# FFN's products in halves, at other addresses, and grouped with the attention's products

## The chip, the core and the metric

The kernel runs on one core of a Trainium2 chip, in one launch. The metric is the device time of a run in microseconds, the median of several runs. Before the change it is 484.53 us (three runs, 483.99 to 485.03). Besides the timed runs there is one profiled execution, with a trace of every instruction; all durations below come from that trace.

## The reference

One transformer layer over x of 4 x 2048 tokens of 256 features, in float32, cut to what is computed:

```python
Q, K, V = x @ W_q.T, x @ W_k.T, x @ W_v.T
# chunks of 32 tokens; mask[i, j] = decay ** (i - j) for i >= j, else 0
S = einsum('bncd,bnkd->bnck', Qc, Kc) * mask
O = einsum('bnck,bnkd->bncd', S, Vc)
x = layernorm(x + ((sigmoid(x @ W_g.T) * O) @ W_o.T + x))
# FFN: integer weights times 1/127, 768 hidden features
gate, up = x @ wg.T, x @ wu.T
x = layernorm(x + (silu(gate) * up) @ wd.T)
```

## The kernel before

**Blocks and passes.** The 8192 tokens are cut into 16 blocks of `TB` = 512. Features lie in `KD` = 2 groups of 128 partitions, hidden features in `KH` = 6 chunks of 128. The main loop (L1173) makes one pass for each of blocks 0 to 13. A pass works on three blocks at once: the FFN of block b, attention's values and output of block n = b + 2, and projections and scores of block m = b + 3. Passes 1 to 12 take the branches marked `late`; passes 0 and 13 take the others, and the last two blocks have code of their own behind the loop.

**Products in parts.** Float32 operands are split into a high part of the type float32r (a float32 format of TensorE) and a rest. FFN's rests are fp16: a chunk of FFN is a sum of high x high (float32r) and rest x rest (fp16) products. They are written in `ffn_pieces` (L912), which returns three functions: the high products, the low products, and one that issues silu on ScalarE (L937) and gives back another that issues the multiplication by the up projection on VectorE (L948), the copy to float32r on ScalarE (`u_hi`, L953) and the rest on GpSimd (`u_lo`, L954). The gate and the up projection of a chunk take a PSUM bank each, two products for each kind and projection: the weights are stationary, 128 x 128, and h's transposed block `hT` moves, 512 columns. All products of FFN's up part stand in one line, L923; `fg<-hT_hi,fg_hi` is a high product of the gate, `fu<-hT_lo,fu_lo` a low one of the up projection. `ffn_up` (L965) calls the three functions for whole chunks.

The attention's four projections (gate `p_g`, value `p_v`, scores `p_y`, output `p_o`) have three float32r terms: high, low, and, after ScalarE has scaled the bank, a third ("gap"). `three` (L535) writes them: for each of two banks the high and the low products and ScalarE's scaling (L542), and later, when the function that it returns is called, the third term and what takes the bank away (`finish`). Two helpers write the products. `feature_major` (L495, its products L501) has stationary weights and moves 512 columns of tokens; it serves `split_gate` (L555, finish is a tanh) and `split_y` (L563, finish is a copy to `yT` on VectorE, L567). `token_major` (L513, L523) has stationary tokens and moves the weights' 256 columns; it serves `split_v` (L571) and `split_out` (L824). FFN's down projection `fdn` (L764, in `project_back_late`, L755) also moves 256 columns of weights against stationary tokens, float32r for the high and fp16 for the low part.

The parts of the tokens come from `pieces_of_tokens` (L464): high on ScalarE, low on GpSimd, gap on VectorE; `token_parts` (L488) calls it and hands back the gap's part as a function. `split_h` (L890) makes `hT_hi` (ScalarE) and `hT_lo` (GpSimd) of a normalized block which `move_h` (L867) has transposed with VectorE and 16 DMAs on SyncE's queue.

The scores (`attn_scores`, L647, products L663) are many products of 128 x 32 tiles of the array, and the values (`attn_values`, L708, products L699) are 64 of 64 x 64 tiles; VectorE then multiplies the values by the gate into `goT` (L718).

**What sets the order.** Nearly every instruction goes through `in_turn`, which keeps the written order on its engine; the order of the calls in the loop's body is the order of work on TensorE, ScalarE and VectorE. PSUM's 8 banks are one ring that is handed out in the written order. Addresses in SBUF come from the tile pools: each pool is one stretch, and the pools follow each other in the order in which they are opened (L101 to L113). In the built program before, every weight's high part lies at an address with remainder 192 modulo 256 bytes, and the tokens' parts (`hT_hi`, `u_hi`, the parts of x and of `goT`) at remainder 0.

TensorE's order in a late pass before the change (numbers are FFN's chunks):

```
low 0, low 1, high 0, high 1 | y: high and low | high 2, low 2 | y: third
high 3, low 3 | scores (L663) | values (L699) | low 4, low 5, high 4
gate: high and low | value: high and low | gate: third | high 5 | value: third
output: high and low | down: high of chunks 0, 1 | output: third | down: high of 2 to 5, low
```

Of the kernel before, what the change touches and what calls it, by code (L numbers as in the profile page):

```python
# [48 lines left out]
F32R = mybir.dt.float32r  # L49
# [5 lines left out]
P = 128  # L55
# [3 lines left out]
TB = 512  # L59
NG = TB // P  # L60
HB = TB // 2
# [15 lines left out]
def kernel(  # L77
# [18 lines left out]
    KD = D // P  # L96
# [2 lines left out]
    assert NB > 3  # L99

    const = ctx.enter_context(tc.tile_pool(name="const", bufs=1))  # L101
    setup = ctx.enter_context(tc.tile_pool(name="setup", bufs=2))
    xin = ctx.enter_context(tc.tile_pool(name="xin", bufs=2))
    work = ctx.enter_context(tc.tile_pool(name="work", bufs=2))
# [5 lines left out]
    sums = ctx.enter_context(tc.tile_pool(name="sums", bufs=1))  # L110
    small = ctx.enter_context(tc.tile_pool(name="small", bufs=8))
    tiny = ctx.enter_context(tc.tile_pool(name="tiny", bufs=1))
    psum = ctx.enter_context(tc.tile_pool(name="psum", bufs=8, space=bass.MemoryType.PSUM))  # L113

    def in_turn(ins):
        tc.keep_in_program_order(ins)

    def bank(name):
        return psum.tile([P, TB], F32, tag="ps", name=name)
# [156 lines left out]
    def integers(w, w_int, name):  # L276

        k, n = w.shape[0] // P, w.shape[1]
        both = [
            const.tile([P, k, n], dtype, tag=f"{name}_{kind}", name=f"{name}_{kind}")  # L280
            for kind, dtype in (("hi", F32R), ("lo", F16))
        ]

        def cast(kind, which=range(len(w_int))):
            for i in which:
                in_turn(nc.scalar.copy(pieces_of(both[kind], i), w_int[i]))

        return both, cast
# [199 lines left out]
    def token_parts(t, name):  # L488
        parts, high, low, difference = pieces_of_tokens(t, name)
        for k in range(KD):  # L490
            high(k)
            low(k)
        return parts, lambda: [difference(k) for k in range(KD)]

    def feature_major(a, b):  # L495

# [347 lines left out]
    def transpose_h(b, h, up=H_UP):  # L844

        up = H_UP / up
        hi = work.tile([P, KD, TB], F32R, tag="hT_hi", name=f"hT_hi_{b}")
        lo = work.tile([P, KD, TB], F16, tag="hT_lo", name=f"hT_lo_{b}")
        for dc in range(KD):
            pt = bank(f"pt_{b}_{dc}")  # L850
            for g in range(NG):
                in_turn(
                    nc.tensor.transpose(
                        pt[:, g * P : (g + 1) * P], h[:, g, dc * P : (dc + 1) * P], ident
                    )
                )
            in_turn(nc.scalar.mul(hi[:, dc, :], pt, up))
            in_turn(
                nc.vector.scalar_tensor_tensor(
                    lo[:, dc, :], pt, up, hi[:, dc, :].bitcast(F32), ALU.mult, ALU.subtract  # L860
                )
            )
        return hi, lo
# [24 lines left out]
        return hT  # L888

    def split_h(b, hT):  # L890
        hi = work.tile([P, KD, TB], F32R, tag="hT_hi", name=f"hT_hi_{b}")
        lo = work.tile([P, KD, TB], F16, tag="hT_lo", name=f"hT_lo_{b}")
        for dc in range(KD):
            whole = hT[:, dc, :, :].rearrange("p q (g t) -> p g q t", g=NG)
            in_order = [
                part[:, dc, :].rearrange("p (g q t) -> p g q t", g=NG, q=NQ)
                for part in (hi, lo)
            ]
            tc.keep_in_program_order(nc.scalar.copy(in_order[0], whole))  # L899
            nc.gpsimd.tensor_tensor(  # L900
                in_order[1], whole, in_order[0].bitcast(F32), ALU.subtract
            )
        return hi, lo
# [4 lines left out]
    def no_more_splits():  # L908
        while late_splits:
            late_splits.pop(0)()  # L910

    def ffn_pieces(b, hT, uT, hc, cols=slice(0, TB)):  # L912

        n = cols.stop - cols.start
        pg = bank(f"fg_{b}_{hc}_{cols.start}")[:, :n]
        pu = bank(f"fu_{b}_{hc}_{cols.start}")[:, :n]
        fresh = [pg, pu]

        def products(kind):
            for i, (pb, w) in enumerate(((pg, fg), (pu, fu))):  # L920
                for dc in range(KD):
                    for part in [cols]:
                        product = nc.tensor.matmul(  # L923
                            pb[:, part.start - cols.start : part.stop - cols.start],
                            lhsT=w[kind][:, dc, hc * P : (hc + 1) * P],
                            rhs=hT[kind][:, dc, part],
                            start=len(fresh) > 1 - i,
                            stop=True,
                            skip_group_check=True,
                        )  # L930
                        in_turn(product)
                        if len(fresh) > 1 - i:
                            fresh.pop()

        def activate():
            s = work.tile([P, n], F32, tag="s", name=f"s_{b}_{hc}")
            in_turn(nc.scalar.activation(s, pg, AF.Silu, scale=SCALE / H_UP))  # L937
            no_more_splits()
            if len(uT[0]) == hc:
                for kind, dtype, tiles in zip(("hi", "lo"), (F32R, F16), uT):  # L940
                    tiles.append(
                        acts.tile([P, TB], dtype, tag=f"u_{kind}", name=f"u_{kind}_{b}_{hc}")
                    )

            def multiply():
                u = work.tile([P, n], F32, tag="u", bufs=3, name=f"u_{b}_{hc}")
                in_steady_turn(
                    nc.vector.scalar_tensor_tensor(u, pu, U_UP / H_UP, s, ALU.mult, ALU.mult)  # L948
                )
                hi, lo = uT[0][hc][:, cols], uT[1][hc][:, cols]  # L950

                def split():
                    in_steady_turn(nc.scalar.copy(hi, u))  # L953
                    in_steady_turn(nc.gpsimd.tensor_tensor(lo, u, hi.bitcast(F32), ALU.subtract))  # L954

                if lagging:
                    late_splits.append(split)
                else:
                    split()

            return multiply

        return lambda: products(0), lambda: products(1), activate
# [209 lines left out]
    for b in range(NB - 2):  # L1173
# [13 lines left out]
        def pieces(hc):  # L1187
            return ffn_pieces(b, hT, uT, hc)
# [3 lines left out]
        if late:  # L1192
            (high_0, low_0, silu_0), (high_1, low_1, silu_1) = pieces(0), pieces(1)
            low_0()
            low_1()
            high_0()
            silu_0()()
            high_1()
            multiply = silu_1()
        else:  # L1200
            if b:
                up_now(b, hT, uT, 0)
            multiply = ffn_up(b, hT, uT, range(1, 2), held=True)
# [11 lines left out]
            multiply()  # L1215
        if not more:
            goT = attn_values(n, sT, v, sg)
        multiply = ffn_up(b, hT, uT, range(2, 3), held=True)
        if b > 1:
            normalize(r_before, *scales_out, range(NG // 2))  # L1220
        multiply()
# [13 lines left out]
        if more:  # L1235
            sT_next = attn_scores(m, yT)
            goT = attn_values(n, sT, v, sg)
            if late:
                (high_4, low_4, silu_4), (high_5, low_5, silu_5) = pieces(4), pieces(5)
                low_4()  # L1240
                low_5()
                go_parts, go_gaps = token_parts(goT, f"go_{n}")
                high_4()
                silu_4()()
                go_gaps()
                sg_next, g_rest = split_gate(m, x_parts)
                v_next, v_rest = split_v(m, x_parts)
                gate = g_rest(hold=True)
                if m + 1 < NB:
                    x_parts, x_high, x_low, x_difference = pieces_of_tokens(  # L1250
                        xTs[m + 1], f"x_{m + 1}"
                    )
                    for k in range(KD):
                        x_high(k)
                high_5()
                multiply = silu_5()
                v_copies = v_rest(hold=True)
                gate()
                multiply()
                if m + 1 < NB:  # L1260
                    for k in range(KD):
                        x_difference(k)
            else:
                multiply = ffn_up(b, hT, uT, range(4, 5), held=True, low_first=True)
                go_parts, go_gaps = token_parts(goT, f"go_{n}")
                cast_fd(1, range(1))
                multiply()
                go_gaps()
                v_next, v_rest = split_v(m, x_parts)
                sg_next, g_rest = split_gate(m, x_parts)  # L1270
                v_rest()
                cast_fd(1, range(1, 2))
                up_with_cast(b, hT, uT, 5, 1, range(2, 3))
# [352 lines left out]
    with tc.If(wide_any > 0, preferred_fallthrough_block=False):  # L1626
# [1 line left out]
        homes = [  # L1628
            pool.tile([P, KD, TB], F32, tag=tag, name=f"wide_{i}")
            for i, (pool, tag) in enumerate(  # L1630
                ((work, "hT_hi"), (work, "hT_hi"), (sums, "x_hi"), (sums, "x_lo"))
            )
        ]
        last_home = work.tile([P, TB], F32, tag="hT_lo", name="wide_last")
# [58 lines left out]
```

## Time and profile before

| | before |
|---|---|
| median of 3 runs | 484.53 us |
| profiled execution, its own time | 485.13 us |
| its span, first to last instruction | 483.5 us |
| granted TensorE clock, mean | 0.997 of full speed |
| ScalarE / VectorE / GpSimd busy | 370.3 / 343.2 / 279.2 us |
| matmul instructions | 3704, of them 736 float32r of 512 columns and 1120 of 256 |

How to read what follows. The page gives, for each engine, the busy time, its share of the span and the number of instructions; then the chain of work that ended last, followed back from the last instruction. The timeline has a line for each run of equal instructions: start in us from the span's start, time to the end of the last one, engine, source line, operation, output<-inputs, tile of the array, shape, type and count; a float32r product is listed as f32. Products overlap in the array: a product's own duration in the trace (some 0.28 us for 256 columns, 0.4 for 512) is longer than the distance from its start to the next one's. So the cost of products on TensorE is read from start to start, and two runs in the timeline overlap by the last product's tail.

### The profile page before, as it was taken

To read this page: it belongs to the slowest core of one execution; us is meant where nothing else is said; L and a number is where in the kernel's file an instruction comes from. 1 tells how busy PE (TensorE), PEld (TensorE's weight loads), DVE (VectorE), ACT (ScalarE), POOL (GpSimd) and SP (SyncE) were. 2 spreads that over 40 slices of the span, in tenths; PEclk is the share of its full clock that TensorE was granted. 3 is DMA by queue.
4 is the path that set the end of the run, shared out by engine and by line. 5 is a ranking of instruction groups with operands and counts; after the bars stand their busy time and mean duration, and the time that the engine had idled before them with its cause. 6 is when DMAs were issued, how large, how long until landed. Compare 5 with 4: busy or idle time off the path is not lost.

```text
span 483.5 us, 12279 instructions
## 1 busy us (share of the span) xinstructions
PE 477.2 (99%) x4760; PEld 380.8 (79%) x4760; DVE 343.2 (71%) x795; ACT 370.3 (77%) x699; POOL 279.2 (58%) x285
## 2 busy tenths in 40 slices
PE   9999999999999999999999999999999999999995
PEld 5788787787978879697787978878697787968674
DVE  4587958776777766858676777866858676677656
ACT  4878788587877778788786887778788786786845
POOL 2835755655655566455655645565455555557764
PEclk9999999999999999999999999999999999999998
DMA  7730321221313114031321313114031211103102
GB/s 258 234 102 21 107 69 46 55 79 31 109 50 118 45 41 137 26 107 49 102 70 33 109 53 115 45 45 131 23 111 50 83 45 35 56 20 113 37 15 82
DMA packets 43323, 36.99 MB, mean 77 GB/s; under 512 B 4864, under 2 KB 39168, under 8 KB 43264
## 3 DMA queue, kind: packets, MB, share of 16 engines
q1 hardware_dynamic: 42144, 35.28, 23.3%
q10 hardware_dynamic: 1120, 0.92, 0.6%
q8 instruction: 38, 0.62, 0.5%
q14 instruction: 21, 0.17, 0.1%
HBM read 20.45 MB, written 8.39 MB: 60 GB/s over the span
## 4 chain that ended last, share of the span: by engine, by line
PE 98%; DMA 1%; DVE 0%; ACT 0%; issue 0%
PE fg L923 18%; PE fu L923 18%; PE fdn L764 13%; PE p_v L523 9%; PE p_y L501 9%; PE p_o L523 9%; PE p_g L501 9%; PE po L699 4%; PE ps L663 2%; PE fdn L1017 2%; PE fdn L1435 1%; PE fdn L745 1%; PE pg L587 1%; PE pa L811 1%; PE pv L629 1%; PE py L608 1%
## 5 line engine op out<-in xcount | busy, mean ns | idle before, releaser
L954 POOL TENSOR_TENSOR u_lo<-u,u_hi 128x512 f16<-128x512 f32 (+1 forms) x98 | 132.7, 1360 | 94.5 <-ACT u_hi L953 94.4
L948 DVE SCALAR_TENSOR_TENSOR u<-fu,s 128x512 f32<-128x512 f32 (+1 forms) x98 | 66.2, 675 | 76.4 <-ACT s L937 59.0
L953 ACT CAST u_hi<-u 128x512 fp32r<-128x512 f32 (+1 forms) x98 | 59.9, 611 | 36.0 <-DVE u L948 36.0
L937 ACT ACTIVATE s<-fg 128x512 f32<-128x512 f32 (+1 forms) x98 | 57.2, 584 | 15.4 <-PE fg L923 15.4
L923 PE MATMUL fg<-hT_hi,fg_hi 128*128 128x512 f32 (+1 forms) x196 | 67.5, 425 | 0.0
L923 PE MATMUL fu<-hT_hi,fu_hi 128*128 128x512 f32 (+1 forms) x196 | 60.2, 388 | 0.0
L923 PE MATMUL fg<-hT_lo,fg_lo 128*128 128x512 f16 (+1 forms) x196 | 58.0, 377 | 0.0
L923 PE MATMUL fu<-hT_lo,fu_lo 128*128 128x512 f16 (+1 forms) x196 | 57.4, 375 | 0.0
L476 POOL TENSOR_TENSOR go_lo<-goT,go_hi 128x512 fp32r<-128x512 f32 x30 | 39.3, 1331 | 14.4 <-ACT go_hi L472 14.4
L476 POOL TENSOR_TENSOR x_lo<-xT,x_hi 128x512 fp32r<-128x512 f32 x30 | 37.5, 1272 | 15.2 <-ACT x_hi L472 15.2
L481 DVE SCALAR_TENSOR_TENSOR go_gap<-go_hi,goT 128x512 fp32r<-128x512 f32 x30 | 45.0, 1540 | 0.8 <-ACT go_hi L472 0.7
L923 PEld LDWEIGHTS fg<-hT_hi,fg_hi 128*128 128x128 f32 x196 | 36.4, 189 | 9.9
L923 PEld LDWEIGHTS fu<-hT_hi,fu_hi 128*128 128x128 f32 x196 | 36.5, 188 | 8.1
L900 POOL TENSOR_TENSOR hT_lo<-hT,hT_hi 128x512 f16<-128x512 f32 x28 | 35.6, 1294 | 7.7 <-ACT hT_hi L899 7.6
L832 DVE TENSOR_TENSOR h<-p_o,x 128x512 f32<-128x512 f32 x30 | 19.3, 685 | 27.4 <-PE p_o L523 25.2
L923 PEld LDWEIGHTS <-fu_lo 128*128 128x128 f16 x196 | 19.2, 98 | 22.2
L764 PE MATMUL fdn<-fd_hi,u_hi 128*128 128x256 f32 x288 | 36.5, 276 | 0.0
L472 ACT ACTIVATE go_hi<-goT 128x512 fp32r<-128x512 f32 x30 | 17.3, 624 | 22.5 <-DVE goT L718 22.5
L764 PEld LDWEIGHTS fdn<-fd_hi,u_hi 128*128 128x128 f32 x288 | 34.4, 188 | 0.0
L764 PE MATMUL fdn<-fd_lo,u_lo 128*128 128x256 f16 x288 | 33.5, 273 | 0.0
L764 PEld LDWEIGHTS <-u_lo 128*128 128x128 f16 x288 | 27.2, 98 | 3.4
L923 PEld LDWEIGHTS <-fg_lo 128*128 128x128 f16 x196 | 15.0, 98 | 18.3 <-issue 9.4
(179 smaller groups left out, 1066.2 us busy)
## 6 DMA issues: line engine op xcount, KB each, us to landing
x<-in_x_dram SPq DMA_DIRECT2D x16, 512.0 KB, 3.8
xT<-in_xT_dram SPq DMA_DIRECT2D x15, 512.0 KB, 4.2
hT<-sq SPq DMA_DIRECT2D x224, 32.0 KB, 1.9
out_dram<-r SPq DMA_DIRECT2D x13, 512.0 KB, 3.1
out_dram<-r SPq DMA_DIRECT2D x7, 128.0 KB, 1.7
fg_int<-in_ffn_gT_dram SPq DMA_DIRECT2D x3, 256.0 KB, 7.2
fu_int<-in_ffn_uT_dram SPq DMA_DIRECT2D x3, 256.0 KB, 6.4
fd_int<-in_ffn_dT_dram SPq DMA_DIRECT2D x3, 256.0 KB, 5.5
```

Source lines behind the costliest of these rows:

```text
L476: in_turn(nc.gpsimd.tensor_tensor(lo[:, k, :], t[:, k, :], whole, ALU.subtract))
L481: nc.vector.scalar_tensor_tensor(gap[:, k, :], whole, -WHOLE, t[:, k, :], ALU.mult, ALU.add)
L501: nc.tensor.matmul(pb, lhsT=a[kind][:, k, i * P : (i + 1) * P], rhs=b[kind][:, k, :], start=kind + k == 0, stop=True, skip_group_check=True,)
L523: nc.tensor.matmul(pb[:, j * D : (j + 1) * D], lhsT=b[kind][:, k, g * P : (g + 1) * P], rhs=a[kind][:, k, :], start=kind + k + j == 0, sto ...
L699: product = nc.tensor.matmul(po[dims, dc * len(groups) + g, :], lhsT=v[rows, g, dc * P + dims.start : dc * P + dims.stop], rhs=sT[rows, g, :],
L764: nc.tensor.matmul(banks[g // per][:, g % per * D : (g % per + 1) * D], lhsT=part[:, g * P : (g + 1) * P], rhs=w, start=first and g % per ...
L900: nc.gpsimd.tensor_tensor(in_order[1], whole, in_order[0].bitcast(F32), ALU.subtract)
L923: product = nc.tensor.matmul(pb[:, part.start - cols.start : part.stop - cols.start], lhsT=w[kind][:, dc, hc * P : (hc + 1) * P], rhs=hT[k ...
L937: in_turn(nc.scalar.activation(s, pg, AF.Silu, scale=SCALE / H_UP))
L948: nc.vector.scalar_tensor_tensor(u, pu, U_UP / H_UP, s, ALU.mult, ALU.mult)
L953: in_steady_turn(nc.scalar.copy(hi, u))
L954: in_steady_turn(nc.gpsimd.tensor_tensor(lo, u, hi.bitcast(F32), ALU.subtract))
```

## The change

It has three parts.

1. *Halves.* The high products of FFN's full chunks are issued as two of 256 columns each, by the new function `halves`; both halves use the same stationary block. The low ones stay at 512. The blocks behind the loop, which already had chunks of 256 columns, issue what they did. In the whole program 376 float32r products of 512 columns become 752 of 256: 4080 matmuls in place of 3704.
2. *Addresses.* The high parts of FFN's gate and up weights move to a new pool `up`, opened behind `const`, and `hT_hi` moves to a new pool `turned`, opened last. In the built program `fg_hi` goes from 43968 to 59392 and `fu_hi` from 53184 to 65536 (remainder 192 to 0 modulo 256 bytes), and the two buffers of `hT_hi` from 118272 and 122368 to 220096 and 224192 (remainder 0 to 192). Every other tile keeps its remainder.
3. *Order.* In the late passes chunk 2's high products go ahead of the y projection, its low ones stay behind it. The gate projection is issued directly behind the values, ahead of low 4 and low 5; chunk 5's high products are issued ahead of the value's third term as before, but the gate's third term comes before high 4:

```
low 0, low 1, high 0, high 1, high 2 | y: high and low | low 2 | y: third
high 3, low 3 | scores | values | gate: high and low | low 4, low 5 | gate: third
high 4 | value: high and low | high 5 | value: third
output: high and low | down: high of chunks 0, 1 | output: third | down: high of 2 to 5, low
```

From high 4 to the down projection's last high product TensorE then has 88 float32r products of 256 columns in a row. ScalarE's order in this stretch goes from

```
go_hi x2, silu 4, u_hi 4, p_g scaling x2, p_v scaling x2, x_hi x2, silu 5, tanh x2, u_hi 5
```

to

```
go_hi x2, p_g scaling x2, tanh x2, silu 4, u_hi 4, p_v scaling x2, silu 5, x_hi x2, u_hi 5
```

On VectorE `go_gap` is issued in two parts, one ahead of chunk 4's multiplication and one behind it, instead of both behind it. GpSimd, SyncE and the DMAs keep their order.

The diff:

```diff
     const = ctx.enter_context(tc.tile_pool(name="const", bufs=1))
+    up = ctx.enter_context(tc.tile_pool(name="up", bufs=1))
...
     tiny = ctx.enter_context(tc.tile_pool(name="tiny", bufs=1))
+    turned = ctx.enter_context(tc.tile_pool(name="turned", bufs=2))
...
+    def home(name, kind):
+        return up if name != "fd" and kind == "hi" else const
...
-            const.tile([P, k, n], dtype, tag=f"{name}_{kind}", name=f"{name}_{kind}")
+            home(name, kind).tile([P, k, n], dtype, tag=f"{name}_{kind}", name=f"{name}_{kind}")
             for kind, dtype in (("hi", F32R), ("lo", F16))
...
-        return parts, lambda: [difference(k) for k in range(KD)]
+        return parts, lambda ks=range(KD): [difference(k) for k in ks]
...
-        hi = work.tile([P, KD, TB], F32R, tag="hT_hi", name=f"hT_hi_{b}")
+        hi = turned.tile([P, KD, TB], F32R, tag="hT_hi", name=f"hT_hi_{b}")
...
+    def halves(cols):
+        return [slice(i, i + HB) for i in range(cols.start, cols.stop, HB)]
...
-                    for part in [cols]:
+                    for part in [cols] if kind else halves(cols):
...
             high_1()
             multiply = silu_1()
+            high_2, low_2, silu_2 = pieces(2)
+            high_2()
...
-        multiply = ffn_up(b, hT, uT, range(2, 3), held=True)
+        if late:
+            low_2()
+            multiply = silu_2()
+        else:
+            multiply = ffn_up(b, hT, uT, range(2, 3), held=True)
...
                 (high_4, low_4, silu_4), (high_5, low_5, silu_5) = pieces(4), pieces(5)
+                go_parts, go_gaps = token_parts(goT, f"go_{n}")
+                sg_next, g_rest = split_gate(m, x_parts)
                 low_4()
                 low_5()
-                go_parts, go_gaps = token_parts(goT, f"go_{n}")
+                g_rest()
                 high_4()
-                silu_4()()
-                go_gaps()
-                sg_next, g_rest = split_gate(m, x_parts)
+                multiply = silu_4()
+                go_gaps(range(1))
+                multiply()
+                go_gaps(range(1, KD))
                 v_next, v_rest = split_v(m, x_parts)
-                gate = g_rest(hold=True)
+                high_5()
+                multiply = silu_5()
+                v_copies = v_rest(hold=True)
                 if m + 1 < NB:
                     x_parts, x_high, x_low, x_difference = pieces_of_tokens(
                         xTs[m + 1], f"x_{m + 1}"
                     )
                     for k in range(KD):
                         x_high(k)
-                high_5()
-                multiply = silu_5()
-                v_copies = v_rest(hold=True)
-                gate()
                 multiply()
```

More of the change, by code (lines that the diff above doesn't have):

```diff
@@ L890, in split_h @@
     def split_h(b, hT):
-        hi = work.tile([P, KD, TB], F32R, tag="hT_hi", name=f"hT_hi_{b}")
+        hi = turned.tile([P, KD, TB], F32R, tag="hT_hi", name=f"hT_hi_{b}")
         lo = work.tile([P, KD, TB], F16, tag="hT_lo", name=f"hT_lo_{b}")
@@ L1630 @@
             for i, (pool, tag) in enumerate(
-                ((work, "hT_hi"), (work, "hT_hi"), (sums, "x_hi"), (sums, "x_lo"))
+                ((turned, "hT_hi"), (turned, "hT_hi"), (sums, "x_hi"), (sums, "x_lo"))
             )
```

## The prediction, and how it was worked out

> **What bounds the kernel now.** I read the page from above: engines, chain, then TensorE's timeline in one pass of the loop.
>
> ```profile
> span 483.5 us, 12279 instructions
> ...
> PE 477.2 (99%) x4760; PEld 380.8 (79%) x4760; DVE 343.2 (71%) x795; ACT 370.3 (77%) x699; POOL 279.2 (58%) x285
> ...
> PE 98%; DMA 1%; DVE 0%; ACT 0%; issue 0%
> ```
>
> TensorE is busy 99% and is 98% of the chain that ended last. Passes are 28.95 us long, with 28.95 us of busy PE in each that the windows view was asked for. So the time is the length of TensorE's stream, and an edit counts by what it does to the spacing of products, or by a wait that it opens. Busy time hides spacing, because products overlap; it is read from start to start. TensorE's timeline in block 5's pass (start, us, ..., count):
>
> ```profile
> 204.38 0.60 PE L923 MATMUL fg<-hT_lo,fg_lo 128*128 128x512 f16 x2
> 204.83 0.59 PE L923 MATMUL fu<-hT_lo,fu_lo 128*128 128x512 f16 x2
> 205.26 0.59 PE L923 MATMUL fg<-hT_lo,fg_lo 128*128 128x512 f16 x2
> ...
> 207.05 0.62 PE L501 MATMUL p_g<-x_hi,wg_hi 128*128 128x512 f32 x2
> 207.51 0.62 PE L501 MATMUL p_g<-x_lo,wg_lo 128*128 128x512 f32 x2
> ...
> 208.43 0.62 PE L501 MATMUL p_g<-x_lo,wg_lo 128*128 128x512 f32 x2
> 208.89 0.63 PE L523 MATMUL p_v<-wv_hi,x_hi 128*128 128x256 f32 x4
> 209.36 0.62 PE L523 MATMUL p_v<-wv_lo,x_lo 128*128 128x256 f32 x4
> ...
> 212.09 0.62 PE L923 MATMUL fu<-hT_hi,fu_hi 128*128 128x512 f32 x2
> 212.56 1.09 PE L523 MATMUL p_v<-wv_gap,x_gap 128*128 128x256 f32 x8
> 213.48 0.62 PE L523 MATMUL p_o<-wo_hi,go_hi 128*128 128x256 f32 x4
> 213.93 0.62 PE L523 MATMUL p_o<-wo_lo,go_lo 128*128 128x256 f32 x4
> ```
>
> Two fp16 products of 512 columns take 204.83 to 205.26, 216 ns each. Two float32r of 512 take 207.05 to 207.51; over longer stretches 229 each. Four float32r of 256 take 213.48 to 213.93: 113.3 each, 226.6 for 512 columns. Entering 256 from 512 costs something: the first four of p_v take 0.47 us, the eight of L523's third term 0.92 (115 each). And 256 columns have a second, slower rhythm; block 2's timeline:
>
> ```profile
> 70.35 1.10 PE L523 MATMUL p_o<-wo_gap,go_gap 128*128 128x256 f32 x8
> 71.30 0.87 PE L745 MATMUL fdn<-fd_hi,u_hi 128*128 128x256 f32 x6
> 72.01 1.48 PE L745 MATMUL fdn<-fd_lo,u_lo 128*128 128x256 f16 x12
> ```
>
> Eight take 0.95 us and six 0.71: 118 each, to the end of the run. In the late passes p_v settles from 118 to 113 after four or five products; here 14 did not. All of these move weights (remainder 192 modulo 256) against stationary tokens (remainder 0). FFN's last half chunks have the remainders the other way round; behind fp16 at 470.19 eight of them ran at 118, behind float32r at 468.93 four at 113.
>
> **The change, part by part.** Twelve passes (blocks 1 to 12) have the reordered branch; I price one, in ns, from the trace's starts.
>
> *Size and remainders.* 376 products of 512 become 752 of 256 with the remainders of p_v, p_o and fdn. At 113.3 each product of 512 gains 229 - 226.6, about 2.5 ns; at 118 it loses 7. So all together -0.9 or +2.6 us: the run decides. The Trainium skill speaks against the split: its page TensorE: Matmul & The Clock Gate, section "Wait — 56ns, not 53.3ns?", gives a warm matmul N/2.4 + 2.5 ns, so each additional one is 2.5 ns of loss, as an estimate 376 x 2.5 = 0.9 us. Its rule fits the fp16 rows here (216 for 512, 109 for 256 at L764) and not the float32r rows (229 and 113), and the rows decide.
>
> *The run.* In the built program a late pass has 88 float32r products of 256 on end (chunk 4, value, chunk 5, value's third term, output, down) and 24 more (chunks 0 to 2).
> - Chunk 4: now 932 behind fp16; then eight of 256 behind four of 512 that follow fp16. Two rows stand so: p_v at 60.95 (910) and p_o at 67.60 (932), both settling; unsettled 944. I take -5.
> - Value, 1830 to 16 x 113.3 = 1814: -16. Chunk 5, 922 to 907: -15. Value's third term, 924 to 907: -17. These are the entries that go.
> - Chunks 0 to 2: now 2766 behind fp16. 24 x 113.3 + 20 for entry = 2741; unsettled 2837. The only float32r run behind 512-column fp16 with 256 columns, fdn at 457.89, kept 118 for its eight. I let eight be slow: 2757, -9.
> - Chunk 3 is alone between 512-column y and fp16: 917 to 910, 932 or 944 by the same rows. I take +10.
>
> *The gate moves up behind the value products L699*, which are 64x64. Today fp16 follows them. Only block 13's pass has float32r there:
>
> ```profile
> 427.96 1.16 PE L699 MATMUL po<-sT,v 64*64 64x64 f32 x64
> 429.05 0.73 PE L923 MATMUL fg<-hT_hi,fg_hi 128*128 128x512 f32 x2
> 429.62 0.62 PE L923 MATMUL fu<-hT_hi,fu_hi 128*128 128x512 f32 x2
> ```
>
> The value products take 1.09 us either way (203.29 to 204.38; 427.96 to 429.05), but the next two products take 569 ns instead of 2 x 229: +110. Two fp16 there take 442 instead of 432: +10. The other rows with float32r behind the small products agree: third terms of y at 27.05 start with 333, y behind scores at 50.78 with 340. So +100 per pass, the largest term. The gate's third term, now behind fp16, costs 0 (y's third terms at 199.61) to +17 (chunk 4 at 205.93): +8.
>
> *Waits.* ScalarE's order changes as well: p_g's scaling and both tanh go ahead of silu 4, and p_v's scaling stands behind u_hi 4. Laid out with the trace's durations, p_g's scaling ends 0.3 us before the gate's third term wants it, and p_v's as far before v's: no stall, without much to spare. Chunk 2's high products delay y by 0.91 us. That makes p_y's second scaling (198.75 now, held by ScalarE) wait for TensorE, some 0.4 us later, and behind it on ScalarE stand u_hi 1 and silu 2, behind those on VectorE u 2 and yT:
>
> ```profile
> 198.23 1.07 ACT L542 ACTIVATE p_y<-p_y 128x512 f32<-128x512 f32 x2
> ```
> ```profile
> 201.03 1.28 DVE L567 COPY yT<-p_y 128x512 f32<-128x512 f32 x2
> ```
>
> yT ends at 202.31 and the score products that read its second half start at 202.68: 0.32 us to spare after 0.05 for the semaphore. A delay of 0.35 to 0.44 uses that up: 0 to 0.12 us of stall; I take 0.03. The output's go_gap split in two around u 4 is needed 3 us later: nothing. POOL, SP and the DMAs keep their order; hT_hi's new address changes no queue.
>
> *Elsewhere.* 22 chunk groups outside the late passes stand between fp16 rows: each -5 settled, +20 at 118. I take +8, together +0.18 us.
>
> **Sum.** Per late pass 100 + 8 - 5 - 16 - 15 - 17 - 9 + 10 + 30 = +86 ns; twelve times, +1.03; with the rest +1.21, rounded to +1.2 us. The profiled execution lasted 485.13 us (span 483.5 and 1.6 around it), so 486.3 by it; it stood 0.6 above the median of the runs, 484.53, and on that I forecast **485.7 us**. With everything settled at once and no wait: 12 x (100 - 22 - 16 - 15 - 17 - 26 - 7) less 0.1 is 0.1 us below nothing. With nothing settling and every wait at its upper end: the gate 117, chunk 4 12, value and chunk 5 58 + 22, v's third term 20, output and down 48 x 4.6 = 221, chunks 0 to 3 71 + 27, yT 120 make 668, twelve times, and 22 x 20: +8.5 us.
>
> **Rivals.**
> 1. *The run never settles* (slower). The 88 products enter from a 512 row, and at 70.35 such an entry kept 118 for 14 products. At 4.6 ns each the run costs 0.4 us a pass. For it: 70.35, 42.16 and 457.89. Against it: 60.95 and 67.60, and in all twelve late passes both entries of p_v settle. All passes alike: about 490 to 493; a part of them, 488.
> 2. *FFN's halves are faster than any float32r row here* (the other side: faster). Two neighbours load the same stationary block, which no 256-column row does now, so the price is open below; the nearest bound is fp16's 109.3. It decides from about 111.5 ns on, where it pays for the gate's 100. At 109.3: 752 x 4 = 3.0 us, and the slow entries (0.4) go: 482.3. Against it: p_v, p_o and fdn, with the same remainders, are all at 113.3.
> 3. *A new wait bites*: yT, p_g or p_v later than laid out by 0.2 us, 12 x 0.2 = 2.4 more: 488.1. For it: three margins of 0.3 or less. Against it: each is from repeated rows.
>
> **Numbers.** Forecast (-0.1 to +2.2) 0.63; rival 1 0.13, rival 2 0.15, rival 3 0.09. A measurement of this kernel tells about 0.2%, 0.97 us, from no change. The forecast's median lies near that edge, so it gives half to slower and half to no change: slower 0.54, same 0.31, faster 0.15. The range reaches from most of rival 2 to the lower part of rival 1: 482.9 to 488.6; the forecast's own is 484.4 to 486.7.
>
> **What would show it.** Right: in TensorE's timeline the gate's first pair behind L699 takes 0.57 us; value, chunk 5, output and down take 0.45 us per four; a late pass is 29.02 to 29.06 us long. Chunks 0 to 2 tell how soon a run settles behind fp16. Wrong: 118 through the 88 (rival 1); chunks at 0.44 per four (rival 2); score products starting more than 0.35 us after the last fp16 row, or a gap before p_g's or p_v's third term (rival 3). The reckoning falls if the entry behind L699 costs a 512-column gate less than it does FFN.

## The result, and the profile after

The changed kernel takes 488.25 us (median of 4 runs, 487.75 to 489.14) against 484.66 before (4 runs, 483.99 to 485.03): 1.0074 of the time, 95% interval 1.0058 to 1.0091, 3.6 us more. The profiled execution lasted 489.14 us, the longest of the four, against 485.13 before. The page of the changed kernel, from above:

```profile
span 487.6 us, 13010 instructions
...
PE 481.2 (99%) x5136; PEld 401.6 (82%) x5136; DVE 321.9 (66%) x795; ACT 371.4 (76%) x699; POOL 279.7 (57%) x285
```

Nothing on the page names a culprit. TensorE is still 99% busy, and 98% of the chain that ended last, with 4.0 us more of busy time for the same arithmetic, and with the 376 products more that the halves make. The granted clock is 0.997 in both traces, so it is not the clock that differs. So the loss lies in the spacing of products and is read from start to start, pass by pass. From one block's score products to the next's a late pass took 28.95 us before (11 of them in the trace, 28.950 to 28.987). After, ten take 29.226 to 29.247 and one 29.600. Those eleven are 3.4 of the 4.1 us by which the span grew; 0.2 lie ahead of the first score product, in code that is the same in both, where the 14 traces of this study scatter by 1.3 us.

TensorE's timeline of the changed kernel in block 5's pass, from chunk 2 to the gate (start, us, ..., count; only starts are used):

```profile
198.39 0.64 PE L933 MATMUL fu<-hT_hi,fu_hi 128*128 128x256 f32 x4
198.87 0.63 PE L507 MATMUL p_y<-x_hi,m_hi 128*128 128x512 f32 x2
...
200.74 0.61 PE L933 MATMUL fg<-hT_lo,fg_lo 128*128 128x512 f16 x2
...
204.45 0.81 PE L669 MATMUL ps<-yT,xT 128*32 128x32 f32 x64
205.19 1.16 PE L705 MATMUL po<-sT,v 64*64 64x64 f32 x64
206.28 0.73 PE L507 MATMUL p_g<-x_hi,wg_hi 128*128 128x512 f32 x2
206.85 0.62 PE L507 MATMUL p_g<-x_lo,wg_lo 128*128 128x512 f32 x2
```

Chunk 2's last four products of 256 take 0.47 to 0.48 us: 118 each, 24 products after the run began. Then something that no late pass showed before: y's eight products of 512 take 1.87 us, 234 each and not 229. The slower rhythm, some 4.5 ns a product, is carried over into another width and other operands. The score products take 0.74 us and took 0.69. The gate's first pair behind the value products takes 0.57. The same products in the kernel before, where y took 1.83 us:

```profile
196.17 0.62 PE L501 MATMUL p_y<-x_hi,m_hi 128*128 128x512 f32 x2
196.63 0.62 PE L501 MATMUL p_y<-x_lo,m_lo 128*128 128x512 f32 x2
...
198.00 0.62 PE L923 MATMUL fg<-hT_hi,fg_hi 128*128 128x512 f32 x2
...
202.60 0.76 PE L663 MATMUL ps<-yT,xT 128*32 128x32 f32 x64
203.29 1.16 PE L699 MATMUL po<-sT,v 64*64 64x64 f32 x64
```

The run from chunk 4 on comes in two kinds. The same timeline, the value's first products in two neighbouring passes:

```profile
94.52 0.64 PE L529 MATMUL p_v<-wv_hi,x_hi 128*128 128x256 f32 x4
95.00 0.63 PE L529 MATMUL p_v<-wv_lo,x_lo 128*128 128x256 f32 x4
...
124.13 0.62 PE L529 MATMUL p_v<-wv_hi,x_hi 128*128 128x256 f32 x4
124.58 0.62 PE L529 MATMUL p_v<-wv_lo,x_lo 128*128 128x256 f32 x4
```

Four products take 0.47 to 0.48 us in the first pass and 0.45 in the second. In the second chunk 4 settled after five products. In the first all 88 stay at 118, to the end of the run; that is the pass of 29.600 us, the only one of the eleven. The code, the addresses and the order are the same in both.

Stage by stage, the median of each stretch over the eleven passes, ns from start to start:

| Stretch of a late pass | before | after | difference | predicted |
|---|---|---|---|---|
| gate behind the values | 1835 | 1956 | +121 | +100 |
| low 4, low 5, gate's third term, chunk 4 | 3584 | 3601 | +17 | +3 |
| value | 1830 | 1813 | -17 | -16 |
| chunk 5 | 922 | 907 | -15 | -15 |
| value's third term | 923 | 907 | -16 | -17 |
| output and high down | 5444 | 5444 | 0 | 0 |
| chunks 0 to 2, high | 2955 | 3019 | +64 | -9 |
| y, high and low | 1831 | 1871 | +40 | 0 |
| low 2 and y's third term | 1789 | 1804 | +15 | 0 |
| chunk 3, high | 917 | 937 | +20 | +10 |
| score products | 693 | 745 | +52 | +30 |

Together about +0.28 us a pass, where I had +0.086.

### The profile page after: what moved, and what is told of

Same layout as the page of the kernel before. It is cut to its first block, busy times and chain, and to the rows that moved or that the text cites. A ratio compares the mean times of both kernels' runs of the same rounds, so it can differ in the third digit from the quotient of the medians.

```text
span 487.6 us, 13010 instructions
## 1 busy us (share of the span) xinstructions
PE 481.2 (99%) x5136; PEld 401.6 (82%) x5136; DVE 321.9 (66%) x795; ACT 371.4 (76%) x699; POOL 279.7 (57%) x285
## 4 chain that ended last, share of the span: by engine, by line
PE 98%; DMA 1%; DVE 0%; ACT 0%; issue 0%
PE fg L933 18%; PE fu L933 18%; PE fdn L770 13%; PE p_g L507 9%; PE p_y L507 9%; PE p_v L529 9%; PE p_o L529 9%; PE po L705 4%; PE ps L669 2%; PE fdn L1027 2%; PE fdn L1452 1%; PE fdn L751 1%; PE pg L593 1%; DMA wg<-in_w_gT_dram 1%; PE pa L817 1%; PE pv L635 1%
## 5 line engine op out<-in xcount | busy, mean ns | idle before, releaser
L964 POOL TENSOR_TENSOR u_lo<-u,u_hi 128x512 f16<-128x512 f32 (+1 forms) x98 | 127.1, 1303 | 99.0 <-ACT u_hi L963 99.0
L933 PE MATMUL fg<-hT_hi,fg_hi 128*128 128x256 f32 x384 | 66.1, 293 | 0.0
L933 PE MATMUL fu<-hT_hi,fu_hi 128*128 128x256 f32 x384 | 60.6, 279 | 0.0
L933 PEld LDWEIGHTS fg<-hT_hi,fg_hi 128*128 128x128 f32 x384 | 55.5, 189 | 5.7
L482 POOL TENSOR_TENSOR go_lo<-goT,go_hi 128x512 fp32r<-128x512 f32 x30 | 45.0, 1519 | 14.1 <-ACT go_hi L478 14.1
L933 PEld LDWEIGHTS fu<-hT_hi,fu_hi 128*128 128x128 f32 x384 | 51.9, 189 | 0.0
L487 DVE SCALAR_TENSOR_TENSOR go_gap<-go_hi,goT 128x512 fp32r<-128x512 f32 x30 | 23.4, 789 | 9.2 <-ACT go_hi L478 9.1
```

The source lines that it names most:

```text
L482: in_turn(nc.gpsimd.tensor_tensor(lo[:, k, :], t[:, k, :], whole, ALU.subtract))
L487: nc.vector.scalar_tensor_tensor(gap[:, k, :], whole, -WHOLE, t[:, k, :], ALU.mult, ALU.add)
L933: product = nc.tensor.matmul(pb[:, part.start - cols.start : part.stop - cols.start], lhsT=w[kind][:, dc, hc * P : (hc + 1) * P], rhs=hT[k ...
```

## The experiments

Theory A, formed from this trace: a run of float32r products that begins with 256 columns behind fp16 keeps the slower rhythm to its end, whatever the width of what follows; addresses play no part; float32r directly behind the value products costs some 110 ns; and the scores wait for yT because chunk 2's high products delay y. Its rival, B: the addresses set the rhythm. Pass lengths below are from score products to score products in one profiled execution of each kernel, ratios are to the kernel before on the same chip, with 95% intervals.

**The parts alone.** First halves without the other two parts:

```diff
-                    for part in [cols]:
+                    for part in [cols] if kind else halves(cols):
```

> The kernel before with FFN's high products in halves; addresses and order as before. Theory A (entry): a float32r run of 256 columns that begins behind fp16 keeps the slow rhythm (118), the slow rhythm costs about 4.6 ns for each product whatever its width, and it lasts until the run ends, 512-column products included; addresses play no part. Then chunks 0 and 1 are 45 ns longer, y 40, chunk 2 18, y's third term 15, chunk 3 20, chunk 4 12, the gate 36; and if value to down stay slow too, another 320: 0.19 to 0.52 us a pass, 487 to 491 us. Theory B (addresses): the old remainders (weights 192, tokens 0) make FFN's halves slow everywhere and the new ones cure that: chunks at 118 each, 512-column y and gate products at their 229, about 0.1 us a pass, 486. Theory C: halves cost nothing, 484.6.

Measured: 486.50 us, 1.0032 (1.0020 to 1.0044), pass 29.05. TensorE's timeline of this kernel:

```profile
225.86 0.63 PE L501 MATMUL p_y<-x_hi,m_hi 128*128 128x512 f32 x2
226.33 0.62 PE L501 MATMUL p_y<-x_lo,m_lo 128*128 128x512 f32 x2
226.79 0.62 PE L501 MATMUL p_y<-x_hi,m_hi 128*128 128x512 f32 x2
```

Chunks 0 and 1 are at 118, as A has it (2072 ns in place of 2030). But y leaves the slower rhythm after its first pair (0.47 us, then 0.46, and 229 each from there), so the rhythm does not last "until the run ends", and B's price, 486, is the nearer one. B is not whole either: chunk 3 settles (911 ns, before 917).

Next the order alone: the changed kernel without halves, and with both pools left out, so that all tiles are where they were.

```diff
-                    for part in [cols] if kind else halves(cols):
+                    for part in [cols]:
...
-        return up if name != "fd" and kind == "hi" else const
+        return const
...
-        hi = turned.tile([P, KD, TB], F32R, tag="hT_hi", name=f"hT_hi_{b}")
+        hi = work.tile([P, KD, TB], F32R, tag="hT_hi", name=f"hT_hi_{b}")
```

> The changed order, with 512-column products and the old addresses. Theory A and my prediction's other terms: the gate behind the 64x64 value products costs 116 ns as in the changed kernel's trace, the score products wait some 48, chunk 2's high products ahead of y gain 8, chunk 4 behind the gate's third term gains 11: +0.145 us a pass of 28.95, 29.10; 12 passes are 1.7 us: about 486.4. If the order's own costs were all of the change's loss, the pass would be 29.23 and the time 488.2; if the order were free, 484.6.

Measured: 487.87 us, 1.0060 (1.0043 to 1.0076), pass 29.22 to 29.25. I had 29.10. By the length of a pass, the order by itself costs as much as the whole change: the gate 121 ns, the scores 91 and the value 54. Its timeline:

```profile
203.08 0.85 PE L667 MATMUL ps<-yT,xT 128*32 128x32 f32 x64
203.87 1.16 PE L703 MATMUL po<-sT,v 64*64 64x64 f32 x64
...
210.49 0.63 PE L527 MATMUL p_v<-wv_hi,x_hi 128*128 128x256 f32 x4
210.96 0.63 PE L527 MATMUL p_v<-wv_lo,x_lo 128*128 128x256 f32 x4
```

The scores take 0.78 us, 91 ns more than before and 39 more than in the changed kernel. There the products between y and the scores are 36 ns longer in sum, and the wait for yT hides just that: what TensorE gains ahead of that wait it gives back in it. From y's end to the end of the wait it is 3.76 us in both. And the value products now enter from chunk 4 where they entered from the gate; all sixteen stay at 118 (1884 ns, before 1830) in all eleven passes.

Then halves and order without the addresses (of the edit above, the lines on `home` and `hi`):

> The changed kernel with the old addresses (halves and order stay). Theory A (entry decides, addresses play no part): chunks 0 to 2 at 118 and y at 233.5 as in the changed kernel, the run from chunk 4 on at 113 in nearly all passes: pass 29.23 us, 488.2. Theory B (the new addresses let the run settle): chunks 4 and 5 at 118 and with them the 88 products of the run, 0.4 us a pass more: 492 to 493.

Measured: 489.78 us, 1.0097 (1.0080 to 1.0114), passes 29.29 and 29.33, one of 29.47. Neither theory. Its timeline:

```profile
210.67 0.62 PE L931 MATMUL fg<-hT_hi,fg_hi 128*128 128x256 f32 x4
211.12 0.62 PE L931 MATMUL fu<-hT_hi,fu_hi 128*128 128x256 f32 x4
211.58 0.64 PE L527 MATMUL p_v<-wv_hi,x_hi 128*128 128x256 f32 x4
212.05 0.64 PE L527 MATMUL p_v<-wv_lo,x_lo 128*128 128x256 f32 x4
```

Chunk 4 is settled (0.45 us per four, so in seven of the eleven passes) and the value products behind it, of the same width and kind, fall back to 0.47. In the changed kernel they do not. What changes at that boundary is which operand lies at which remainder: hT_hi moves at 0 against weights at 192, then the weights move at 192 against tokens at 0. A's "no part" is wrong.

And the addresses alone, the two pools of the change put into the kernel before:

> The kernel before with hT_hi and FFN's gate and up weights at their new addresses; order and 512-column products as before. The last two runs showed FFN's halves at 120 ns, and never settled, where both operands have the same remainder (192 and 192, or 0 and 0), and 113 or 118 where they differ, whichever way round. Theory R (only equal or different counts): here they differ as before, 512 columns stay at 229, the pass at 28.95 to 28.98 us, 484.7 to 485.1. Rival (a boundary at which the sides change places, from y or the gate to FFN and back, is a new entry at 512 columns too): y 40 ns, the gate 36 and chunk 2 10 longer, 29.04, 485.8.

Measured: 486.21 us, 1.0025 (1.0015 to 1.0035), pass 29.07. Its timeline:

```profile
224.84 0.63 PE L928 MATMUL fg<-hT_hi,fg_hi 128*128 128x512 f32 x2
225.31 0.63 PE L928 MATMUL fu<-hT_hi,fu_hi 128*128 128x512 f32 x2
```

FFN's own products of 512 take 0.47 us a pair at the new addresses, 233.5 each, in every chunk (before 229), and y and the gate take 19 and 13 ns more. Neither R nor its rival: it is the size of the rival's loss in other places.

**Which address.** The changed kernel with only hT_hi moved (`home` returns `const`), then with only FFN's weights moved (`hi` comes from `work`):

> The changed kernel with only hT_hi at its new address (remainder 192); FFN's weights back at 192. The run without either address change showed the value products at 118 behind chunk 4's at 113, y at 229 behind slow chunks; the changed kernel shows the value at 113 and y at 233.5. Theory M (a boundary where the remainder of the moving operand changes is a new entry, the stationary one's plays no part): here hT_hi moves with 192 as the value's weights do, so value 1814 ns, y 1871, pass 29.23, 488.2. Theory S (the stationary operand's remainder decides): value about 1887 and chunk 5 940, y 1840, pass 29.29, 489.3.

> The changed kernel with only FFN's gate and up weights at their new addresses (remainder 0); hT_hi back at 0. Theory M (the moving operand's remainder decides): value about 1887 ns, chunk 5 940, y 1840, pass 29.29, 489.3. Theory S (the stationary one's): value 1814, y 1871, pass 29.23, 488.2.

Measured: 493.84 us, 1.0180 (1.0162 to 1.0199), pass 29.65 to 29.67; and 490.15 us, 1.0103 (1.0085 to 1.0121), pass 29.35. By the pass, both theories fall in both runs. The timeline with hT_hi alone moved:

```profile
214.62 0.64 PE L932 MATMUL fg<-hT_hi,fg_hi 128*128 128x256 f32 x4
215.10 0.64 PE L932 MATMUL fu<-hT_hi,fu_hi 128*128 128x256 f32 x4
```

and with the weights alone moved:

```profile
226.39 0.64 PE L932 MATMUL fg<-hT_hi,fg_hi 128*128 128x256 f32 x4
226.87 0.64 PE L932 MATMUL fu<-hT_hi,fu_hi 128*128 128x256 f32 x4
```

In these two kernels both operands of FFN have the same remainder, 192 in the first and 0 in the second. Then four products take 0.48 us, 119 to 120 each, and are never settled (chunk 5 of the second kernel, short and behind settled products, takes 0.47); in the first even the rest of the run, whose operands differ, stays at 118 to its end. So it is neither operand by itself but the pair.

For y, theory M was right in both runs: 1871 ns with hT_hi moved, 1837 with the weights moved. That holds in all the kernels. Behind FFN's halves with hT_hi at its old address y takes 1837 to 1842 ns, and with hT_hi at the new one 1871 (1853 where chunk 2 is not ahead of it). So the slower rhythm crosses into the whole of y only with the tokens' move; at the old address it ends within y.

To try the pair on products that had always been at 113, fd_hi alone was moved on the kernel before, so that it has u_hi's remainder (in a pool `down` of its own behind `const`):

```diff
+    def home(name, kind):
+        return down if name == "fd" and kind == "hi" else const
```

> The kernel before with fd_hi alone moved, from remainder 192 to 0, which u_hi, the down projection's stationary operand, has too. Nothing else moves. Theory R (equal remainders slow every float32r product of 256 columns): the 24 high products of the down projection in a late pass take 120 each in place of 113.3, 160 ns, and the eight of the output's third term between them 118, 37 more: 29.15 us a pass; with the blocks outside 487.3. Rival (it is FFN's up part alone, where two neighbours share a stationary block): 28.95, 484.7.

Measured: 486.77 us, 1.0034 (1.0025 to 1.0044), pass 29.09 in seven of eleven. Its timeline:

```profile
215.18 1.10 PE L768 MATMUL fdn<-fd_hi,u_hi 128*128 128x256 f32 x8
216.12 1.09 PE L527 MATMUL p_o<-wo_gap,go_gap 128*128 128x256 f32 x8
217.05 2.06 PE L768 MATMUL fdn<-fd_hi,u_hi 128*128 128x256 f32 x16
```

and in the kernel before:

```profile
215.29 1.07 PE L764 MATMUL fdn<-fd_hi,u_hi 128*128 128x256 f32 x8
216.20 1.07 PE L523 MATMUL p_o<-wo_gap,go_gap 128*128 128x256 f32 x8
217.10 1.98 PE L764 MATMUL fdn<-fd_hi,u_hi 128*128 128x256 f32 x16
```

Eight take 0.94 us, and sixteen 1.90 to the next row, 118 to 119 each, where they took 0.907 and 1.818: 137 ns a pass with the output's third term between them. A rival is that each change of pair only begins the slower rhythm of 118 anew. Against it, the last seven distances among the sixteen are 120 ns in every pass, as in FFN's halves above. The rule holds outside of FFN's up part; its size was 30% less than I took, because the first eight of a run stay near 118. (The four longer passes wait up to 0.15 us at their score products, and in two of them p_v stays at 118; no run says why.)

**What begins a run.** The changed kernel with chunk 0 at 512 columns:

```diff
-                    for part in [cols] if kind else halves(cols):
+                    for part in [cols] if kind or (hc == 0 and b > 0) else halves(cols):
```

> The changed kernel, but chunk 0's high products stay at 512 columns in the passes from block 1 on, so that the run of chunks 0 to 2 enters with four products of 512 behind fp16. Theory A: the 512s settle in two or three products, as they did before; chunks 1 and 2 then settle within five products (1833 ns for 16 in place of 1887), chunk 0 takes 1114 in place of 1132 and y 1831 in place of 1871: 0.11 us a pass less, 29.12; about 486.9. Theory B, or one in which the moving tokens of hT_hi themselves are slow: chunks 1 and 2 stay at 118, y at 233.5, pass 29.22, 488.

Measured: 488.15 us, 1.0072 (1.0055 to 1.0088), pass 29.21 to 29.24. No gain: chunk 0 takes 1126 ns, chunks 1 and 2 stay at 118, y at 234. A's remedy fails; with addresses_alone in hand, chunk 0 at 233.5 was itself in the slower rhythm.

**The order's two prices.** Chunk 4's low products ahead of the gate, so that fp16 follows the values:

```diff
+                low_4()
                 sg_next, g_rest = split_gate(m, x_parts)
-                low_4()
                 low_5()
```

> The changed kernel with chunk 4's four low products moved ahead of the gate, so that fp16 and not float32r follows the 64x64 value products; nothing else moves. Theory A (float32r behind the value products costs 110 ns, as the two traces show it): from the values' end to the gate's third term's end 4620 ns become 8 x 216 + 12 x 229 and some 55 for the changes of type, 4530: 0.09 us a pass less, 29.14, and 12 x 0.09 = 1.1 us: 487.2. Rival: the first gate product pays for its own start wherever it stands (its tokens or its bank), the pass stays at 29.23 and the time at 488.2.

Measured: 487.29 us, 1.0048 (1.0030 to 1.0066), pass 29.10 to 29.15, with one of 29.49 whose whole run stayed at 118. As A has it: from the values' end to the gate's end four fp16 and eight float32r products take 2.71 us, 11 ns more than 4 x 216 + 8 x 229, in place of the gate's 121. (A float32r product behind fp16 is recorded some 190 ns early, while its weights, which take 190, begin to load; so a stretch across that boundary is only read as a whole.)

Chunk 2's high products back behind y:

```diff
-            high_2, low_2, silu_2 = pieces(2)
-            high_2()
...
         if late:
+            high_2, low_2, silu_2 = pieces(2)
+            high_2()
             low_2()
```

> The changed kernel with chunk 2's high products back behind y's high and low ones. Theory A (they push y 0.9 us later, and yT is what the score products wait for): the score products take 692 ns again in place of 744; chunk 2's products behind y stay in the slow rhythm (940), y stays slow (1871): 0.05 us a pass less, 29.18, 487.6. Rival: the wait comes from ScalarE's new order or from the longer chunks, and the scores stay at 740.

Measured: 487.12 us, 1.0050 (1.0034 to 1.0066), pass 29.13 in nine of eleven (29.19 and 29.31 in the others). The score products take 693 ns again: the wait was y's delay. Another 50 ns come from runs that start otherwise: y takes 1853 ns (1871), the gate's third term and chunk 4 2025 (2051).

**A better version?** All three losses taken back (halves in chunks 4 and 5 of the late passes only, low 4 first, high 2 behind y):

```diff
-                    for part in [cols] if kind else halves(cols):
+                    for part in halves(cols) if not kind and hc >= 4 and 0 < b < NB - 3 else [cols]:
```

> The changed kernel with its three measured losses taken back: chunk 4's low products first behind the value products, chunk 2's high products behind y again, and halves only in chunks 4 and 5 of the late passes (the others 512 columns, all at the new addresses). Theory A: the gains on value, chunk 5 and the value's third term stay (48 ns), the additional change of type at the gate costs 25 and chunk 4's entry 11: 28.94 us a pass, 484.5. If 512-column products at the new addresses lose at y and the gate as the rival of the run on addresses has it: 29.02, 485.5.

Measured: 485.75 us (12 runs), 1.0019 (1.0009 to 1.0028), pass 29.01 to 29.03 in eight of eleven, one of 29.44. The rival's number: FFN's 512-column products pay at the new addresses (0.47 us a pair), and so does y behind them (1850 ns, before 1831). At the old ones value and chunk 5 stayed near 118 behind chunk 4 in ten of eleven passes (no_addresses); this repaired order at the old addresses was not tried.

And with all 512-column products together (halves in chunk 5 only):

```diff
-                sg_next, g_rest = split_gate(m, x_parts)
                 low_4()
                 low_5()
-                g_rest()
+                sg_next, g_rest = split_gate(m, x_parts)
                 high_4()
                 multiply = silu_4()
+                g_rest()
```

> Like the run repaired, but all float32r products of 512 columns behind the values' fp16 stand together (low 4, low 5, gate, high 4 at 512 columns, the gate's third term), and halves are left in chunk 5 alone, between the value's products: one change of type and one of width in place of two and three. Theory A: 16 to 32 ns a pass less than before: 28.92 to 28.94 us, 484.2 to 484.5; with a new entry where chunk 4's sides differ from the gate's, some 25 more: 28.96.

Measured in the profiled execution: 29.05 us a pass; the run is settled from the fifth value product on, but chunk 4 at the new addresses takes 0.47 a pair and the gate's third term behind it 931 ns. The median of six runs is 488.70 us, 1.0078 (1.0064 to 1.0091). The profiled execution was by far the shortest, 486.58; the other five took 488.69 to 489.17. Runs of 80 products that stay at 118 in some six passes would make those 2.1 us, but no trace of such an execution was taken, so that is argued and not shown. Neither version beats the kernel before.

## Why the prediction was right in sign and too small

Slower was forecast, and 488.25 lies inside the range, though beyond the forecast's own 484.4 to 486.7: +1.2 us became +3.6. That the range held is partly luck: up there it was meant for rival 1 (488) and rival 3 (488.1), and neither is what happened. The prediction's own sign of being right, a late pass of 29.02 to 29.06 us, failed: it is 29.23.

*Right, by term.* The entries in the run: -48 forecast, -48 measured, each of the three within 1 ns. The gate behind the 64x64 values: 100, taken mostly from one pair of rows in block 13's pass; 121 measured in the table, and low4_first shows that it is the neighbour's price. Ten of the difference are a slip of the sum: it took 10 off because fp16 would no longer stand behind the values, but low 4 behind the gate starts with 442 ns as well. The mechanism of the yT wait was right link by link; on ScalarE (first fence) and VectorE of the changed kernel, with the idle time ahead of each and what ended it in brackets:

```profile
200.93 0.58 ACT L548 ACTIVATE p_y<-p_y 128x512 f32<-128x512 f32 x1 [0.35 <-PE p_y L507]
```
```profile
202.62 0.69 DVE L958 SCALAR_TENSOR_TENSOR u<-fu,s 128x512 f32<-128x512 f32 x1 [1.76 <-ACT s L947]
203.23 1.28 DVE L573 COPY yT<-p_y 128x512 f32<-128x512 f32 x2
```

p_y's second scaling waits for TensorE; u_hi 1 and silu 2 follow on ScalarE (201.43 and 201.93), and for that silu u 2 waits on VectorE, ahead of yT. yT ends at 204.51 while the scores begin at 204.45. I took 30 ns; the table shows 52, and high2_back that they go with chunk 2's place.

*Wrong.* The step was "I let eight be slow: 2757, -9" for chunks 0 to 2, beside "unsettled 2837". All 24 stayed at 118 in all eleven passes: +64. They do so at the old addresses too (no_addresses), so there the halves behind fp16 are enough. My bounds held that case, but I chose from the row that suited the hope of settling, and took the length from the only run that the trace had there, which ended at eight because it had no more. A second step was not in the sum at all, in no bound: that a rhythm crosses into neighbours of another width. I priced y at nothing, since its code and operands are unchanged; it took 40 more, and its third term 15. Of these 40 halves_alone shows 11; the rest comes with hT_hi's new address. Chunk 3 took 20 for my 10, chunk 4 with the gate's third term 17 for 3. These five are 152 of the 195 ns that I missed; the gate (21) and the scores (22) are the rest.

I also held remainders to be free as long as they are those of rows at 113. p_v, p_o and fdn did show 113 with that pairing, and chunk 5 in the run takes 113 with it. But the price goes with the width: at 512 columns the same pairing costs FFN 4.5 ns a product (addresses_alone, +0.11 us a pass), and a change of pairing inside a run can begin the slower rhythm anew (no_addresses). Rival 1 was real, in one pass of the eleven traced. Rival 2 fell: no row of four or more float32r products of 256 columns in any run is below 113 ns each. Rival 3 fell: the one new wait is yT's, 52 ns where the rival asked for 0.2 us.

The account by parts is not a sum: halves alone +0.10 us a pass, addresses alone +0.11, order alone +0.28, all three +0.28. With the order in place the halves cost 0.06 more (no_addresses), and the addresses give 0.05 back. One reason that parts do not add up is the wait for yT: whatever lengthens TensorE's stretch between y and the scores, 36 ns here, vanishes in it.

The Trainium skill, page TensorE: Matmul & The Clock Gate, section "Step-by-step: what each phase is for", gives TensorE two read ports and says that loading the next weights "doesn't steal SBUF read bandwidth from the running matmul". The rows here show that, for float32r, addresses count all the same: 113 ns with one pair of remainders and 119 to 120 with two equal ones, for the same instructions. That the two reads are what meets there is a guess; no run separates it from other causes.

## What to carry to other kernels

Where an engine is busy all the time, measure from start to start, and price a regrouping by its boundaries: every change of type, width or tile size is a term, and so is the rhythm that it hands to unchanged neighbours. A state seen for eight products in a trace where the run had eight is known for no longer run; take the bad end unless some row shows it ending. Moving a tensor to another address is an edit with a price of its own: run it alone before it is bundled.

## What the runs showed of the hardware

Float32r products of 128x128 by 256 columns follow each other in 113.3 ns or 118, and by 512 in 229 or 233.5 on average: a second rhythm about 4.5 ns longer per product, at both widths. It begins at boundaries and ends after 3 to some 20 products, or not before the run does; identical passes of one execution differ in it (29.23 and 29.60 us). Where both operands lay at the same remainder modulo 256 bytes, the products went over to a third one, 120 ns for 256 columns, in FFN's halves and in the down projection. Only the remainders 0 and 192 were tried, at one or two places for each tile, so that 256 is the modulus, or that it is the remainder and not the place, is not shown; nor is what ends the slower rhythm. A float32r group of 512 columns directly behind 64x64 products costs about 110 to 136 ns once (block 13's pass, and tokens_address); behind fp16 it costs some 10 to 16.
